# A two-stage fused kernel with twelve of its second-stage inputs turned by VectorE blocks and on-chip copies, and its first tile turned before its mean is known

## The chip, the cores and the metric

The kernel runs on one NeuronCore of one Trainium2 chip. The metric is the device time of one execution in microseconds, as the median of several runs. The profile is of one further execution, and its span is what the profiler saw between the first and the last instruction.

The engines are named as the profile names them: PE is TensorE's matmul stream and PEld its weight loads, DVE is VectorE, ACT is ScalarE, POOL is GpSimd, SP is SyncE. SP does no arithmetic here: it issues transfers from one queue, in order. POOL issues the indirect transfers (gathers of rows and scatters of rows). SBUF is the working memory of 128 partitions, and PSUM the memory into which PE writes.

## The reference, cut to what matters

There are 2048 tokens (4 x 512) of width 512, all in float32. A token's id chooses one of four experts by the thresholds 6250, 12500 and 18750. Each expert is one 512 x 512 matrix, which serves as gate, up and down matrix alike:

```
h  = layernorm(x)                       # no learned scale
g  = silu(h @ Wg[e].T);  u = h @ Wu[e].T
x  = x + tanh(g_xattn) * ((g * u) @ Wd[e].T)
```

The second stage is a feed-forward network over all tokens of the new x, with a router over eight experts, of which two are chosen:

```
h      = layernorm(x)
probs  = softmax(h @ wr.T); gates, idx = top 2, normalised
f      = silu(silu(h @ w1.T) @ w3.T) @ w2.T
out    = zeros; for k in 0, 1: out[idx[:, k]] += gates[:, k] * f
x      = x + tanh(g_ffn) * out
```

The index here is the expert's number, 0 to 7, and it is used as a row number. So the whole second stage adds up into rows 0 to 7 of the output, and the order in which tokens stand in it does not matter.

## The kernel before, in words

**Positions.** The kernel reads all token ids and works out, with DVE and small matmuls, a place for each token such that tokens of one expert lie together. `tok` (lines 274 to 278, sixteen small matmuls) gives for each of 17 passes of 128 places the token that sits there. `from_row` (L286) is the table for the gathers. `later`, `stepped` and `which` (L287 to L300) give for each unit its expert's matrix. `row_tables` (L308 to L323) gives the table for the scatters. While this runs, `busy` keeps PE occupied with matmuls whose result is not used.

**Passes.** Thirteen passes (0 to 12) hold 128 tokens of one expert each. Four more (13 to 16) hold four units of 32 places, each unit with its own matrix. A matrix is 1 MB; `load` issues it from SP into one of seven buffers (pool `mp`). SP first reads the expert's number from a table in SBUF (`which0` for the first pass, `held` for the others; `held` is a copy which POOL makes of `which`).

For each pass the work is: `gather` (POOL, L389); `centre` (DVE: moments of the row, mean taken off, L340 to L401); `turn_in` (PE transposes the 128 x 512 tile in four 128 x 128 pieces into PSUM, ACT copies it to `hT`); `up` (PE: z from hT and m, eight matmul records of 128 x 512; ACT: silu with the row's scale; DVE: the product g, L467); `turn_mid` (PE transposes g, ACT copies it to `gT`); `down` (PE: y; DVE adds the input row, L481; POOL scatters it to the output); `norms` (DVE: moments of the new row, L340, the inverse square roots of this row and of a later pass's input row with nine small instructions each, L355 to L373, and the scaled row `h_f`, L505); `turn_out` (PE transposes h_f into `tp_f`, ACT copies it to `hT2`, L515, or for passes 13 to 16 in four pieces at places read from a table, L527). `hT2` holds the second stage's input, features on partitions.

**The order of the work** is written out by hand; there is no scheduler. Each engine runs its own list in the order of the code. One turn i of the main loop (L876 to L909) issues `up` of pass i, `turn_in` of i + 1, `centre` of i + 2, `gather` and `load` of i + 3, `down` of i - 1, `turn_out` of i - 2, `norms` of i - 1, and `turn_mid` of i (positions in the list `order`, L383).

**The second stage** is taken in two blocks b of 1024 tokens. `sums_of_hT(b)` issues the router's products `lg` (PE, L699, two halves), then on DVE the difference T1, the 32 x 32 block transposes of the two `lg` (L710), and T2 to T4. `first_layer` is Strassen's scheme with seven products (X, Y, Z, L622), `second_layer` the products v (L730). These are cut into steps of 3.4 us of PE work each, and `step()` puts one step into the stream of passes. From turn 11 on there are two steps in a turn. Both `lg` and both X products lie in the pool `ps_x`, which has two PSUM buffers: X of a block takes the buffer of the first `lg` and can start only when that `lg` has been transposed by DVE. Before the change, `sums_of_hT(0)` stands at the end of turn 10, and the first step comes in turn 11, after that turn's z and y.

Of the kernel before, what the change touches and what calls it, by code (L numbers as in the profile page):

```python
# [19 lines left out]
P = 128  # L20
# [5 lines left out]
def tile_gated_moe_ffn(  # L26
# [39 lines left out]

    nc = tc.nc
# [17 lines left out]
    mp = ctx.enter_context(tc.tile_pool(name="mp", bufs=7))  # L85
    xp = ctx.enter_context(tc.tile_pool(name="xp", bufs=5))
# [13 lines left out]
        "idt", "pad", "psum", "padded", "lanes", "inpass",  # L100
# [12 lines left out]
    def load_w(src, name):  # L113
        w = ct_([P, KC, src.shape[1]], F32, name)
        nc.sync.dma_start(w, src.rearrange("(k p) f -> p k f", p=P))
        return w
# [148 lines left out]
    at_lane(0)  # L265
    what = ct_([P, NP, NJ], F16, "what")
# [6 lines left out]
    at_lane(1)  # L273
# [10 lines left out]
    busy(21)  # L284
# [20 lines left out]
    def row_tables():  # L305
# [18 lines left out]
            first, psum, float(-(NB - 1) * TB), float(TB), ALU.add, ALU.min  # L324
# [3 lines left out]
    hT2 = [ct_([P, KC, TB + (Q if b == NB - 1 else 0)], F32, f"hT2_{b}") for b in range(NB)]  # L328
# [9 lines left out]
    def moments(xt, name):  # L338
        st = small.tile([P, 6], F32, tag="st", name=f"st_{name}")
        nc.vector.bn_stats(st, xt)  # L340
        mv = small.tile([P, 2], F32, tag="mv", name=f"mv_{name}")
        nc.vector.bn_aggr(mv, st)
        return mv

    def inverse_roots(mvs_, names):


        n = range(len(names))

        def new(tag):  # L350
            return [small.tile([P, 1], F32, tag=tag, name=f"{tag}_{name}") for name in names]

        v, r, q, w, rs = new("v"), new("r"), new("q"), new("w"), new("rs")
        for i in n:
            nc.vector.tensor_scalar_add(v[i], mvs_[i][:, 1:2], EPS)  # L355
        for i in n:
            nc.vector.tensor_scalar(
                r[i].bitcast(I32), v[i].bitcast(I32), -0.5, float(0x5F3759DF), ALU.mult, ALU.add
            )
        for i in n:  # L360
            nc.vector.scalar_tensor_tensor(q[i], r[i], v[i], r[i], ALU.mult, ALU.mult)
        for i in n:
            nc.vector.tensor_scalar(w[i], q[i], 0.375, -1.25, ALU.mult, ALU.add)
        for i in n:
            nc.vector.tensor_scalar(w[i], w[i], q[i], 1.875, ALU.mult, ALU.add)
        for i in n:
            nc.vector.tensor_mul(r[i], r[i], w[i])
        for i in n:
            nc.vector.scalar_tensor_tensor(q[i], r[i], v[i], r[i], ALU.mult, ALU.mult)
        for i in n:  # L370
            nc.vector.tensor_scalar(q[i], q[i], -0.5, 1.5, ALU.mult, ALU.add)
        for i in n:
            nc.vector.tensor_mul(rs[i], r[i], q[i])  # L373
        return rs
# [8 lines left out]
    order = [0, 1, 2, 3, 4, 5, NF, 6, 7, 8, NF + 1, 9, 10, NF + 2, 11, 12, NF + 3]  # L383
    assert sorted(order) == list(range(NP))
    xs, x1s, mvs, rss, hs, hTs, gTs, gs, hs2, mats = {}, {}, {}, {}, {}, {}, {}, {}, {}, {}

    def gather(p):
        xt = xp.tile([P, D], F32, tag="x", name=f"x_{p}")
        nc.gpsimd.indirect_dma_start(  # L389
            out=xt,  # L390
            out_offset=None,
            in_=x,
            in_offset=bass.IndirectOffsetOnAxis(ap=from_row[:, p : p + 1], axis=0),
        )
        xs[p] = xt

    def centre(p):

        mvs[p] = moments(xs[p], f"a{p}")
        hs[p] = work.tile([P, D], F32, tag="h", bufs=4, name=f"h_a{p}")  # L400
        nc.vector.tensor_scalar(hs[p], xs[p], mvs[p][:, 0:1], None, ALU.subtract)  # L401

    def scale(*ps):
        for p, rs in zip(ps, inverse_roots([mvs.pop(p) for p in ps], [f"a{p}" for p in ps])):
            rss[p] = rs
# [6 lines left out]
    def first_in(p):  # L412

        st = small.tile([P, 6], F32, tag="st", name=f"st_a{p}")
        nc.vector.bn_stats(st, xs[p])
        mvs[p] = small.tile([P, 2], F32, tag="mv", name=f"mv_a{p}")
        nc.vector.bn_aggr(mvs[p], st)
        hTs[p] = work.tile([P, KC * P], F32, tag="hT", bufs=2, name=f"hT_{p}")
        n = D // 2
        for i in range(2):  # L420
            h = work.tile([P, n], F32, tag="h", bufs=4, name=f"h_a{p}_{i}")
            nc.vector.tensor_scalar(
                h, xs[p][:, i * n : (i + 1) * n], mvs[p][:, 0:1], None, ALU.subtract
            )
            tp = ps_tp.tile([P, n], F32, tag="tp", name=f"tp_a{p}_{i}")
            for k in range(n // P):
                nc.tensor.transpose(tp[:, k * P : (k + 1) * P], h[:, k * P : (k + 1) * P], ident)
            nc.scalar.copy(hTs[p][:, i * n : (i + 1) * n], tp)  # L428

    def load(p):  # L430

        n0, n = (p, 1) if p < NF else (NF + (p - NF) * G, G)
        mats[p] = []
        for i in range(n0, n0 + n):
# [9 lines left out]
            mats[p].append(m)  # L444
# [47 lines left out]
    def norms(p_in, p_out):  # L492
# [4 lines left out]
        xt = x1s.pop(p_out)  # L497
        mv = [moments(xt, f"f{p_out}")]
        names = [f"f{p_out}"]
        if p_in is not None:  # L500
            mv.append(mvs.pop(p_in))
            names.append(f"a{p_in}")
        rs = inverse_roots(mv, names)
        h = work.tile([P, D], F32, tag="h", bufs=4, name=f"h_f{p_out}")
        nc.vector.tensor_scalar(h, xt, mv[0][:, 0:1], rs[0], ALU.subtract, ALU.mult)  # L505
        hs2[p_out] = h
        if p_in is not None:
            rss[p_in] = rs[-1]

    def turn_out(p):  # L510

        tp = transposed(hs2.pop(p), f"f{p}").rearrange("p (k t) -> p k t", k=KC)
        if p < NF:
            b, t = divmod(p, TB // P)
            nc.scalar.copy(hT2[b][:, :, t * P : (t + 1) * P], tp)  # L515
            return
        for i in range(G):
            n = (p - NF) * G + i
            place = NF * P + n * Q - (NB - 1) * TB
# [3 lines left out]
                min_val=min(place - E * (Q - 1), TB),  # L523
                max_val=min(place, TB),
                skip_runtime_bounds_check_because="its place less at most E (Q - 1) pads, at most TB",
            )
            nc.scalar.copy(hT2[NB - 1][:, :, bass.ds(at, Q)], tp[:, :, i * Q : (i + 1) * Q])  # L527
# [47 lines left out]
    def sums_of_w1():  # L575

        h = D // 2
        a11, a12 = w1[:, 0:2, 0:h], w1[:, 2:4, 0:h]
        a21, a22 = w1[:, 0:2, h:D], w1[:, 2:4, h:D]
        ss = [ffp.tile([P, 2, h], F32, tag=f"S{i}", name=f"S{i}") for i in range(1, 5)]  # L580
# [10 lines left out]
    def sums_of_hT(b):  # L591
# [3 lines left out]
        b11, b12 = hT2[b][:, 0:2, 0:HB], hT2[b][:, 0:2, HB:TB]  # L595
        b21, b22 = hT2[b][:, 2:4, 0:HB], hT2[b][:, 2:4, HB:TB]
        ts = [ffp.tile([P, 2, HB], F32, tag=f"T{i}", name=f"T{i}_{b}") for i in range(1, 5)]
# [7 lines left out]
    def first_layer(b):  # L605
# [14 lines left out]
        def product(out_ps, a, bb, c, start):  # L620
            for k in range(2):
# [3 lines left out]
                    bb[:, k, :],  # L625
# [66 lines left out]
    def logits(b, half):  # L692
# [3 lines left out]
        for k in range(KC):  # L696
            cols = hT2[b][:, k, half * HB : (half + 1) * HB].rearrange("p (t c) -> p t c", t=TT)
# [127 lines left out]
    last = {b: max(i for i, p in enumerate(order) if min(p // (TB // P), NB - 1) == b) for b in range(NB)}  # L825
# [20 lines left out]
    load(order[0])  # L846
    gather(order[0])
    one = slice(order[1], order[1] + 1)
    nc.gpsimd.tensor_copy(held[0:1, one], which[0:1, one])
    load(order[1])  # L850
    for i in range(1, 5):
# [3 lines left out]
    first_in(order[0])  # L855
    scale(order[0])
    centre(order[1])
    scale(order[1])
    load(order[2])
    nc.sync.dma_start(gates[:, 0:1], g_xattn.to_broadcast([P, 1]))  # L860
    nc.sync.dma_start(gates[:, 1:2], g_ffn.to_broadcast([P, 1]))
    load(order[3])
    up(order[0], inside=lambda: turn_in(order[1]))
    centre(order[2])
# [8 lines left out]
    load(order[4])  # L873
# [89 lines left out]
```

## Time and profile before

| quantity | value |
|---|---|
| median time of 3 runs | 279.15 us (279.06 to 279.7) |
| the profiled execution's own time | 277.53 us |
| its span | 275.8 us |
| PE busy | 266.6 us (97% of the span) |
| DVE busy | 148.7 us (54%) |
| ACT busy | 69.3 us (25%) |
| PE transposes of h_f (tp_f), 68 records | 10.4 us in all |
| DMA moved | 42.54 MB |

The span leaves out 1.7 us of the execution's own time, and this execution was 1.6 us under the median of the three runs. Differences worked out in the span are therefore set against the span, and the result is then placed on the median. PE's matmul records overlap (a record of 0.595 us follows the last at 0.43 us), so the pieces of the chain of waits, which are counted from end to end, give the true cost of a piece of PE work.

### The profile page before, as it was taken

What the parts mean: (1) busy time and instruction counts of PE and PEld (TensorE: products, weight loads), DVE (VectorE), ACT (ScalarE), POOL (GpSimd) and SP (SyncE); (2) the same over time, 40 slices, a digit from 0 to 9 for tenths busy, and PEclk for the clock granted to TensorE, in tenths of its full rate; (3) what the DMA queues carried; (4) which work ended last, traced back from release to release, by engine and by line L of the source; (5) the groups of instructions that cost most, each with busy time, mean ns of one, the idle gap of its engine ahead of it and who ended that gap; (6) DMA issues with size and microseconds to landing.
All of it is one profiled execution on the core that took longest, in us unless ns stands there. A gap on an engine that the chain in (4) does not pass through costs nothing.

```text
span 275.8 us, 3562 instructions
## 1 busy us (share of the span) xinstructions
PE 266.6 (97%) x1173; PEld 125.4 (45%) x1173; DVE 148.7 (54%) x593; ACT 69.3 (25%) x134; POOL 39.3 (14%) x63
## 2 busy tenths in 40 slices
PE   5889999999999999999999999999999999999994
PEld 2445455544355454444344444534245444344362
DVE  6677877777888769918263481516253620711000
ACT  2022232232232231223143232312113233311120
POOL 6520122221122211211110010101010000000000
PEclk9999999999999999999999999999999999999999
DMA  0697998545669996697304084001000000000000
GB/s 1 217 354 277 408 402 334 173 155 206 228 225 402 389 409 258 173 398 264 112 26 166 2 312 180 38 0 40 0 12 2 0 0 1 0 0 2 0 0 2
DMA packets 20722, 42.54 MB, mean 154 GB/s; under 512 B 2143, under 2 KB 2207, under 8 KB 20704
## 3 DMA queue, kind: packets, MB, share of 16 engines
q1 hardware_dynamic: 17952, 33.66, 34.0%
q0 software_dynamic: 2720, 8.65, 8.3%
q8 instruction: 9, 0.15, 0.2%
q14 instruction: 9, 0.07, 0.1%
q10 hardware_dynamic: 32, 0.01, 0.0%
HBM read 38.10 MB, written 4.47 MB: 154 GB/s over the span
## 4 chain that ended last, share of the span: by engine, by line
PE 94%; DVE 2%; DMA 2%; issue 1%; ACT 0%; DVEq 0%
PE z L453 22%; PE y L453 21%; PE v L730 20%; PE X L622 10%; PE Y L622 5%; PE tp_f L380 3%; PE tp_a L380 3%; PE tp_g L380 3%; PE Z L622 2%; PE acc L742 1%; PE lg L699 1%; DMA x<-in_x_dram,from_row 1%; DMA idt<-in_ids_dram 1%; PE accT L758 1%; PE o L814 0%
## 5 line engine op out<-in xcount | busy, mean ns | idle before, releaser
L453 PE MATMUL z<-m,hT 128*32 128x512 f32 (+1 forms) x232 | 61.8, 595 | 0.2 <-ACT hT L428 0.2
L453 PE MATMUL y<-m,gT 128*32 128x512 f32 (+1 forms) x232 | 61.4, 594 | 0.0
L730 PE MATMUL v<-w,s 128*128 128x512 f32 (+1 forms) x136 | 57.3, 570 | 0.0
L730 PEld LDWEIGHTS v<-w,s 128*128 128x128 f32 x136 | 25.0, 190 | 27.2 <-issue 26.7
L453 PEld LDWEIGHTS z<-m,hT 128*32 128x32 f32 (+1 forms) x232 | 22.6, 146 | 29.5 <-issue 28.1
L453 PEld LDWEIGHTS y<-m,gT 128*32 128x32 f32 (+1 forms) x232 | 22.6, 146 | 27.8 <-issue 27.8
L482 POOL DMA_INDIRECT out_dram<-x,to_row x17 | 17.2, 1011 | 84.9 <-DVE x L481 82.7
L389 POOL DMA_INDIRECT x<-in_x_dram,from_row x17 | 16.7, 984 | 77.5 <-DVE h_a L401 22.9
L467 DVE SCALAR_TENSOR_TENSOR g<-z,rs_a,g 128x512 f32<-128x512 f32 x17 | 12.7, 750 | 27.1 <-ACT g L466 27.0
L466 ACT ACTIVATE g<-z,rs_a 128x512 f32<-128x512 f32 x17 | 11.7, 687 | 51.3 <-PE z L453 51.3
L481 DVE SCALAR_TENSOR_TENSOR x<-y,tg,x 128x512 f32<-128x512 f32 x17 | 12.7, 749 | 16.9 <-PE y L453 16.8
L738 ACT ACTIVATE s<-v 128x512 f32<-128x512 f32 (+1 forms) x17 | 9.7, 572 | 41.9 <-PE v L730 41.9
L515 ACT COPY hT<-tp_f 128x512 f32<-128x512 f32 x13 | 7.6, 587 | 43.5 <-PE tp_f L380 43.5
L340 DVE BATCH_NORM_STATS2 st_a<-x 128x6 f32<-128x512 f32 x16 | 11.0, 688 | 7.5 <-DMA x<-in_x_dram,from_row 7.5
L622 PE MATMUL X<-T,S 128*128 128x512 f32 x32 | 15.0, 592 | 0.0
L380 PEld LDWEIGHTS tp_f<-ident,h_f 128*128 128x128 f32 x68 | 8.2, 141 | 10.2 <-issue 10.2
L340 DVE BATCH_NORM_STATS2 st_f<-x 128x6 f32<-128x512 f32 x17 | 11.8, 695 | 0.6
L380 PEld LDWEIGHTS tp_a<-ident,h_a 128*128 128x128 f32 x64 | 7.7, 140 | 9.4 <-issue 9.1
L640 DVE TENSOR_TENSOR s<-X,c 128x512 f32<-128x512 f32 x4 | 2.8, 692 | 16.2 <-PE X L622 16.2
L473 ACT COPY gT<-tp_g 128x512 f32<-128x512 f32 x17 | 10.0, 586 | 5.3 <-PE tp_g L380 5.3
L380 PE MATMUL tp_f<-ident,h_f 128*128 128x128 f32 x68 | 10.4, 276 | 0.0
L380 PE MATMUL tp_g<-ident,g 128*128 128x128 f32 x68 | 10.2, 273 | 0.0
(165 smaller groups left out, 271.6 us busy)
## 6 DMA issues: line engine op xcount, KB each, us to landing
m<-in_ctxT_dram SPq DMA_DIRECT2D x29, 1024.0 KB
w<-in_w1T_dram SPq DMA_DIRECT2D x1, 1024.0 KB
w<-in_w3T_dram SPq DMA_DIRECT2D x1, 1024.0 KB
w<-in_w2T_dram SPq DMA_DIRECT2D x1, 1024.0 KB
x<-in_x_dram,from_row POOLq DMA_INDIRECT x17, 6.2
out_dram<-x,to_row POOLq DMA_INDIRECT x17, 6.1
wr<-in_wrT_dram SPq DMA_DIRECT2D x1, 64.0 KB
x_first<-out_dram SPq DMA_DIRECT2D x4, 4.0 KB
```

Of the source, the lines that this page charges most:

```text
L340: nc.vector.bn_stats(st, xt)
L380: nc.tensor.transpose(tp[:, k * P : (k + 1) * P], h[:, k * P : (k + 1) * P], ident)
L389: nc.gpsimd.indirect_dma_start(out=xt, out_offset=None, in_=x, in_offset=bass.IndirectOffsetOnAxis(ap=from_row[:, p : p + 1], axis=0),)
L453: nc.tensor.matmul(out_ps[i * n : (i + 1) * n, :], lhs[:, k * P + i * n : k * P + (i + 1) * n], m[:, k, :], start=(k == 0), stop=(k == KC ...
L466: nc.scalar.activation(g, z, AF.Silu, scale=rs)
L467: nc.vector.scalar_tensor_tensor(g, z, rs, g, ALU.mult, ALU.mult)
L473: nc.scalar.copy(gT, tp)
L481: nc.vector.scalar_tensor_tensor(xt, y, tg[:, 0:1], xt, ALU.mult, ALU.add)
L482: nc.gpsimd.indirect_dma_start(out=out, out_offset=bass.IndirectOffsetOnAxis(ap=to_row[:, p : p + 1], axis=0), in_=xt, in_offset=None, bou ...
L622: nc.tensor.matmul(out_ps, a[:, k, c * P : (c + 1) * P], bb[:, k, :], start=start and k == 0, stop=k == 1, skip_group_check=True,)
L730: nc.tensor.matmul(v, s1[:, k, c_b + t * P : c_b + (t + 1) * P], w3[:, k, c0 : c0 + n], start=(k == 0), stop=(k == KC - 1),)
L738: nc.scalar.activation(s2, v, AF.Silu)
```

## The change

Twelve of the seventeen passes (0 to 11) no longer have their second-stage input transposed by PE. In their place:

- ACT makes the scaled row h_f (`norm_out`) from a scale and a shift that DVE prepares; before, DVE made it.
- DVE transposes h_f in 32 x 32 blocks into a staging area (`turn_set`, one instruction for each pass). The staging areas are the two halves of `s1` for passes 0 to 3 and 4 to 7, and the buffer of `w2` for passes 8 to 11.
- SP then issues 16 copies within SBUF for each set of four passes (`exchange`), each of 32 partitions x 2 KB, which bring the blocks to the partitions where they belong. That makes 48 copies.
- `hT2` becomes three tiles for 512 tokens each, and a fourth that is filled by PE and ACT as before (passes 12 to 16).

The first pass's tile is transposed by PE as gathered. Meanwhile DVE sums each row, one matmul spreads the sums over all partitions, and DVE takes the mean off behind the transposition, in two halves. Its gather has a table of its own (`tok0`, `from_row0`), worked out ahead of the table for the other passes.

Also moved: the inverse roots are worked out for two columns at once in eleven instructions; `order` has the passes of four units later; `load` fills buffers as passes free them (`load_free`) and not three passes ahead; `xp` has six buffers, not five; `h` has three, not four; w1 is loaded one turn later, w3 in turn 12, w2 in turn 16; `sums_of_hT(0)` stands at the end of turn 11 with its first step right behind it, and turns 13 and 15 have a third step; one sum of w1 is written over its source; `busy(21)` is `busy(11)`.

```diff
+    what0 = ct_([P, NJ], F16, "what0")
+    nc.vector.scalar_tensor_tensor(what0, inpass, 0.0, number, ALU.is_equal, ALU.mult)
+    at_lane(1)
+    tok0 = ps_x.tile([P, 1], F32, tag="x", name="tok0")
+    for j in range(NJ):
+        nc.tensor.matmul(tok0, atlane[j // H][:, :, j % H], what0[:, j : j + 1], ...)
+    from_row0 = ct_([P, 1], I32, "from_row0")
+    nc.vector.tensor_scalar(from_row0, tok0, -1.0, 0.0, ALU.add, ALU.max)
     what = ct_([P, NP, NJ], F16, "what")
...
-    at_lane(1)
...
-    busy(21)
+    busy(11)
...
-    order = [0, 1, 2, 3, 4, 5, NF, 6, 7, 8, NF + 1, 9, 10, NF + 2, 11, 12, NF + 3]
+    order = [0, 1, 2, 3, 4, 5, 6, 7, 8, NF, 9, 10, NF + 1, 11, NF + 2, 12, NF + 3]
...
     def first_in(p):
+        raw = work.tile([P, KC * P], F32, tag="h", bufs=3, name=f"raw_{p}")
         for i in range(2):
...
+                nc.tensor.transpose(tp[:, k * P : (k + 1) * P], xs[p][:, c : c + P], ident)
+            nc.scalar.copy(raw[:, i * n : (i + 1) * n], tp)
+        total = small.tile([P, 1], F32, tag="total", name="total")
+        nc.vector.tensor_reduce(total, xs[p], AX.X, ALU.add)
+        spread = ps_y.tile([P, P], F32, tag="y", name="spread")
+        nc.tensor.matmul(spread, total.to_broadcast([P, P]), ident, start=True, stop=True)
+        for i in range(2):
+            nc.vector.scalar_tensor_tensor(hTs[p][:, half]..., spread..., -1.0 / D, raw[:, half]...,
+                ALU.mult, ALU.add)
+        mvs[p] = moments(xs[p], f"a{p}")
...
     def norms(p_in, p_out):
+        rs = inverse_roots(mv[:, 0:n, 1], f"f{p_out}")
+        if p_out < NS:
+            nc.vector.scalar_tensor_tensor(shift, mv[:, 0, 0:1], -1.0, rs[:, 0:1], ALU.mult, ALU.mult)
+            scaled[p_out] = rs[:, 0:1], shift
+            return
         nc.vector.tensor_scalar(h, x1s.pop(p_out), mv[:, 0, 0:1], rs[:, 0:1], ALU.subtract, ALU.mult)
...
+    def norm_out(p):
+        nc.scalar.activation(h, x1s.pop(p), AF.Identity, bias=shift, scale=rs)
+
+    def turn_set(p):
+        b, i = divmod(p, 4)
+        nc.vector.transpose(
+            turned_set(b).rearrange("p q (k i t) -> p k q i t", i=4, t=Q)[:, :, :, i, :],
+            hs2.pop(p).rearrange("p (k q t) -> p k q t", k=KC, q=4),
+        )
+
+    def exchange(b):
+        for q in range(4):
+            for g in range(G):
+                nc.sync.dma_start(
+                    hT2[b][q * Q : (q + 1) * Q, g].rearrange("p k c -> p (k c)"),
+                    turned_set(b)[g * Q : (g + 1) * Q, q, :],
+                )
...
     gather(order[0])
     one = slice(order[1], order[1] + 1)
+    gather(order[1])
     nc.gpsimd.tensor_copy(held[0:1, one], which[0:1, one])
-    load(order[1])
-    for i in range(1, 5):
+    load(1)
+    for i in range(2, 5):
         gather(order[i])
...
     for i in range(2, NP + 2):
+        before_last = order[i - 2]
         if i < NP:
             up(order[i])
         if i + 1 < NP:
             turn_in(order[i + 1])
+        if before_last < NS:
+            norm_out(before_last)
         if i + 2 < NP:
             centre(order[i + 2])
         if i + 3 < NP:
             gather(order[i + 3])
-            load(order[i + 3])
+        if before_last in (7, 11):
+            turn_set(before_last)
+        if before_last == 7:
+            exchange(1)
         if i <= NP:
             down(order[i - 1])
-        turn_out(order[i - 2])
+        load_free(i)
+        if before_last == 11:
+            exchange(2)
+        if before_last >= NS:
+            turn_out(before_last)
+        step()
         if i <= NP:
             norms(order[i + 2] if i + 2 < NP else None, order[i - 1])
-        step()
         if i > NP:
             step()
...
         if i < NP:
             turn_mid(order[i])
-        for b in range(NB):
-            if last[b] == i - 2:
-                hT_sums[b] = sums_of_hT(b)
-                running.append(ffn(b))
-        if last[0] != i - 2:
+        if i == 11:
+            hT_sums[0] = sums_of_hT(0)
+            running.append(ffn(0))
+        if i == NP + 1:
+            hT_sums[1] = sums_of_hT(1)
+            running.append(ffn(1))
+        step()
+        if before_last in hs2:
+            turn_set(before_last)
+            if before_last == 3:
+                exchange(0)
+        if i in (13, 15):
             step()
```

NS is 12, the number of passes that go the new way. `load_free(i)` loads, in the order of the units, as many matrices as there are buffers that passes before turn i have used up.

## Prediction

> **What bounds the kernel now.** I read the page first, then the chain of waits in order of time, then the timelines at the three places that the change touches: the start, the first `lg`, the last `lg`. The page:
>
> ```profile
> span 275.8 us, 3562 instructions
> PE 266.6 (97%) x1173; PEld 125.4 (45%) x1173; DVE 148.7 (54%) x593; ACT 69.3 (25%) x134; POOL 39.3 (14%) x63
> PE 94%; DVE 2%; DMA 2%; issue 1%; ACT 0%; DVEq 0%
> ```
>
> PE carries 94% of the chain. In time order the chain is PE's own list from 15.44 us (first z) to 271.3 us, piece after piece without a hole. So a PE piece removed there is worth its full length, and a wait put there costs its full length. First, the end of turn 10, chain and then DVE's timeline:
>
> ```profile
> 101.51 0.44 PE tp_f L380 x4
> 101.94 0.44 PE tp_g L380 x4
> 102.38 1.88 PE lg L699 x64
> 104.26 3.63 PE z L453 x8
> ```
>
> ```profile
> 101.79 0.74 DVE L481 SCALAR_TENSOR_TENSOR x<-y,tg,x 128x512 f32<-128x512 f32 x1
> 105.43 0.54 DVE L505 TENSOR_SCALAR h_f<-x,mv_f,rs_f 128x512 f32<-128x512 f32 x1
> 105.89 1.22 DVE L598 TENSOR_TENSOR T<-hT 128x1024 f32<-128x1024 f32 x1
> 107.03 0.50 DVE L710 STREAM_TRANSPOSE lt<-lg 128x128 f32<-128x128 f32 x2
> ```
>
> PE has finished `lg` at 104.26, but DVE transposes it only at 107.03, because the norms and T1 stand ahead of it. Nobody waits: the X that needs that PSUM buffer comes at 112.49, after a z, a tp_a and a y. The last `lg`, all engines:
>
> ```profile
> 207.24 0.60 PE L380 MATMUL tp_f<-ident,h_f 128*128 128x128 f32 x4
> 207.68 3.60 PE L730 MATMUL v<-w,s 128*128 128x512 f32 x8
> 209.22 0.27 ACT L527 COPY hT<-tp_f 128x128 f32 x1 [0.16 <-ACT hT L527]
> 209.52 1.23 DVE L598 TENSOR_TENSOR T<-hT 128x1024 f32<-128x1024 f32 x1 [5.32 <-ACT hT L527]
> 211.21 1.95 PE L699 MATMUL lg<-hT,wr 128*32 128x128 f32 x64
> ```
>
> A step of v covers the four ACT copies and T1. The start:
>
> ```profile
> 8.88 0.18 DVE L286 TENSOR_SCALAR from_row<-tok 128x17 int32<-128x17 f32 x1 [0.74 <-PE tok L276]
> 10.50 0.18 POOL L849 COPY held<-which 1x1 int32<-1x1 int32 x1
> 11.16 0.39 SPq L443 DMA_DIRECT2D m<-in_ctxT_dram  x1
> 15.44 2.84 PE L453 MATMUL z<-m,hT 128*128 128x512 f32 x6 [0.24 <-ACT hT L428]
> 19.44 0.30 PEld L453 LDWEIGHTS z<-m,hT 128*128 128x128 f32 x2 [0.69 <-ACT hT L410]
> ```
>
> The second pass's matrix is issued at 11.16; the trace has its completion at 19.33, 8.2 us later, amid four gathers. Its hT was ready at 19.35. So z of the second pass (19.70, that is 22.28, the start of tp_g, less six records at 0.43) began with the arrival of its matrix: hT is no later, and no earlier.
>
> [...] 303 ns for 128x128 f32 (L710). [...] The 8 KB of ids took 1.74 us from issue to use, but loads amid gathers take far longer (8.2 us above; gathers a median 6.2). [...] the page's clock row shows full speed throughout[...].
>
> **The change part by part** (against the profiled 275.8).
>
> *PE transposes removed.* Twelve passes x 0.437 us (the tp_f pieces; the 0.59 behind a y of four units moves to the next piece) = -5.24.
>
> *What replaces them, in the turns.* ACT: a copy of 0.59 goes, an activation of 0.69 with a scale (row L466) comes; ACT is 25% busy, nothing. DVE: h_f (0.54) goes, a block transpose comes. No row has 128x512 with a scattered output; between four times 303 = 1.2 us and 512 elements at the pace of h_f, 0.55 us; I take 0.6. Count a turn from the end of y: 0.07 to wake, product 0.77, statistics 0.73 + 0.22, roots 2.16 (nine alone take 1.90 at 201.75 to 203.65; two fused ones become two plain ones each: + 2 x (2 x 0.19 - 0.25)), shift 0.2, a sum of w1 0.62, transpose 0.6: 5.4. The next g waits for silu, 0.44 + 3.44 + 0.75 = 4.6 after the same y, ends at 6.15, and PE wants it at 7.76. So the turn has 1.6 us to spare, and even 1.2 us for the transpose costs nothing. Without this cover, each 0.1 over costs 0.1 in twelve turns.
>
> *Copies.* 48, on SP. Rows of direct issues are 0.28 to 0.49; 16 x 0.37 = 6 us a set. Queued behind are matrices. The tight one is set 1, in the turn in which pass 13 is z. From that z's end E: DVE is through with its transpose at E + 3.5 (silu 0.7, product 0.75, centre 1.4, transpose 0.6), SP with the copies at E + 9.5; the buffers of pass 13 come free only at E + 11.9. Pass 14 wants its matrices at E + 25.9. [...] Hidden. Bound above: rival B.
>
> *Stall 1, at the first X.* Its step now comes directly behind `lg` (end of turn 11). From y's end DVE needs 0.07 + 0.77 + 0.73 + 0.22 + 2.16 + 0.2, then T1 1.14, first transpose 0.30, PE's wake 0.04: 5.63 us. PE has tp_f 0.44, tp_g 0.44, lg 1.88 = 2.76. It waits 2.87, of which 0.19 is the delay that any matmul behind `lg` had before (3.63 against 3.44): +2.7. Behind it T2 to T4 and the add of Z are through before the next g; no further stall.
>
> *Stall 2, at the last `lg`.* Turns 11, 13 and 15 used up the steps, so nothing stands between the last tp_f and `lg`. Copies end 1.65 us after tp_f (207.84 to 209.49), then 0.03 + T1 1.14 + transpose 0.30 + 0.04: X at 3.16, where PE has 1.88 of `lg`. Wait 1.28, less 0.19: +1.1.
>
> *The start.* x_0: `tok0` begins at 7.3 and not 7.85, its gather at 8.8 and not 9.35, the rows arrive at about 12.4. But DVE now waits for PE twice, so `from_row` falls at 10.2 (+1.3), and the tables end at 13.0 and not 11.8: the row sum starts there, 13.65, spread 14.15, first half 14.6, z at 14.6 and not 15.44. Gain 0.8, if the second pass's z could follow. It needs its matrix: `which` + 1.3, and the gather of the second pass now stands ahead of the copy on POOL (0.97), so SP issues at 12.4 and not 11.16. The ramp then meets the gathers of passes 2 to 4 at their thickest (16.5 to 18.5 us). Bounds for its landing: 18.5 (5.2 us from issue were seen for the first matrix + 0.9) to 20.6 (8.2 us). I take 19.8: z of the second pass 0.45 later than before: +0.45. Bounds -0.8 and +1.2.
>
> *The rest* (sixth x buffer, third h buffer, w1 to w3 later, order of units): no PE wait follows from the lists of instructions and their waits. Bounds 0 to +0.5, taken at 0.
>
> Sum: -5.24 + 2.7 + 1.1 + 0.45 = -1.0, span 274.8. On the median: 279.15 - 1.0 = **278.2 us**.
>
> **The rivals.**
>
> *A. The start keeps its gain.* The second matrix lands by 18.5, since it may have been slowed by the gather of pass 1, which now runs ahead of it. For: the first matrix, alone, took 5.2 us. Against: three gathers still come on top. Start -0.8 in place of +0.45: time 276.9. Chance 0.2.
>
> *B. The copies hold up SP (slower).* The built program has SP wait before each copy for the transfer eight places earlier. If a copy takes 8 us to land, as the second matrix did, SP's pace is 1.0 us a copy, not 0.37. Set 1 then ends at E + 19.5, four matrices at E + 31.9, wanted at E + 28.6 with stall 1: +3.3, span 278.1, time 281.5. It decides from 0.8 us a copy, a landing of 6.4 us. For: gathers have a median of 6.2. Against: in slices 13 to 15 DMA has room. Chance 0.15.
>
> *C. The two stalls do not come* (DVE's order lets `lg` be transposed earlier): 274.4. Against: DVE's list has T1 and the norms ahead of it. Chance 0.05.
>
> *D. Something small everywhere:* transposes over 1.6 us, x rows late, PE slowed behind gaps: 279 to 280.5. Chance 0.1.
>
> **How the numbers follow.** The forecast case has 0.5, its own range 277.4 to 279.0. Within 0.3% (0.84 us, about what a measurement of this kernel can tell) is 278.31 to 279.99. Faster: A 0.2, C 0.05, a little over half of the forecast 0.27: 0.52. Same: the rest of the forecast 0.23, half of D 0.05, a mild B 0.02: 0.30. Slower: B 0.13, D 0.05: 0.18. Range 276.7 to 280.6: it leaves out C and the worse part of B.
>
> **What would show it.** Right: the first tp_f is that of pass 13, in turn 11; a hole of 2 to 3 us in PE ahead of the first X, released by DVE L813; a wait of about 1.1 us in two parts at the last `lg`; z of the second pass near 20.1; no PE wait on a matrix elsewhere. Wrong: PE waiting for m in the turn of pass 14 (B), a first X at once behind `lg` (C), tp_g waiting for g (DVE full), or a clock row below full.

## The result, and the profile after

The changed kernel takes 283.98 us as the median of five runs (281.43 to 287.51), where the kernel before takes 279.15 us. The ratio is 1.0146, with a 95% interval of 1.0116 to 1.0177; it leaves out the run of 287.51 us, which is 2.2% above the fastest and counts as slow. So the change made the kernel slower by 1.5%, where the prediction had 278.2 us. The profiled execution after took 283.98 us, with a span of 282.3 us (before 275.8). Single executions of one variant lie up to some 4 us from one another (e4: 279.98 to 283.88), and where their clocks differ (e2), 278.5 to 278.83 us goes with a mean granted clock of 0.996, and 280.32 to 282.73 with 0.98 to 0.986. So ratios carry their intervals, and each is to runs of the kernel before on the same chip. The clock is given as a share of full speed; "half clock" is a granted clock of 0.50, and a "hole" is a stretch in which PE waits.

The page after: busy time, PE's slices, the granted clock, the chain's shares.

```profile
PE 268.4 (95%) x1133; PEld 122.1 (43%) x1133; DVE 150.2 (53%) x510; ACT 71.9 (25%) x134; POOL 39.4 (14%) x63
...
PE   5889999999999996699999999999999999999994
...
PEclk9799999999999999979999999999999999999998
...
PE 86%; DMA 9%; DVE 1%; SPq 1%; issue 1%; POOL 0%; ACT 0%; ACTq 0%; POOLq 0%
```

PE's row has a hole in slices 16 and 17 (106 to 120 us), the clock row has a 7 right behind it, and DMA carries 9% of the chain (before 2%). The timeline of PE there (start, duration, engine, line, work, and in brackets the idle time ahead and what ended it):

```profile
102.52 3.60 PE L510 MATMUL y<-m,gT 128*128 128x512 f32 x8
...
112.09 1.98 PE L725 MATMUL X<-hT,w 128*128 128x512 f32 x4 [1.46 <-DVE lt L813]
...
115.72 1.05 PE L510 MATMUL z<-m,hT 128*32 128x512 f32 x4
117.45 1.05 PE L510 MATMUL z<-m,hT 128*32 128x512 f32 x2 [0.67 <-DMA m<-in_ctxT_dram]
120.16 5.23 PE L510 MATMUL z<-m,hT 128*32 128x512 f32 x26 [1.67 <-DMA m<-in_ctxT_dram]
```

Two things stand one behind the other. The first X comes 5.95 us after the end of y (106.14 in the chain of waits). Then z of pass 14 waits for its third and for its fourth matrix, and its last 26 records take 5.23 us. In all, this z takes from 115.72 to 125.38, 9.66 us where a z of four units takes 3.57. The stretches of four microseconds (PE, PEld, DVE, ACT and POOL busy, granted clock, DMA share, GB/s) say why the last part is slow:

```profile
112.00:116.00 4.00, 3.91 (x10) 1.58 (x12) 3.71 (x6) 0.59 (x1) 0.00 (x0) 1.00 1.04 401
116.00:120.00 4.00, 1.82 (x6) 0.14 (x2) 0.59 (x1) 0.00 (x0) 0.00 (x0) 1.00 1.04 388
120.00:124.00 4.00, 3.84 (x24) 0.97 (x25) 0.00 (x0) 0.00 (x0) 0.00 (x0) 0.57 0.90 334
```

DMA runs full here (a share of 1.02 from 106 to 112 us, 1.04 from 112 to 120), so what can make the matrices late is when they were asked for, and how many bytes are in the way; the experiments separate the two. And behind the holes the clock falls to half (0.50 from 120.0 to 123.4 us). SP's queue, and its line for the copies (min/median/max in ns):

```profile
90.49 11.21 SPq L605 DMA_DIRECT2D hT<-s  x16
102.48 3.62 SPq L492 DMA_DIRECT2D m<-in_ctxT_dram  x4
```

```profile
L605 SPq DMA_DIRECT2D hT<-s x32: 507/589/1754, 64.1 to 101.1; - x32
```

The 16 copies of the second set hold SP from 90.49 to 101.7 us. The first matrix of pass 14 takes the buffer of pass 8, whose last reader y ends at 90.3; the other three take buffers of pass 13, free at 98.2. All four are asked for only from 102.48 on. Without these copies (run e2 below), SP asks for the first at 90.51 and for the second at 98.37:

```profile
90.51 8.23 SPq L492 DMA_DIRECT2D m<-in_ctxT_dram  x2
```

The other two places, the last lg and the start:

```profile
215.76 0.60 PE L404 MATMUL tp_f<-ident,h_f 128*128 128x128 f32 x4
...
219.54 1.98 PE L725 MATMUL X<-hT,w 128*128 128x512 f32 x4 [0.42 <-DVE lt L813]
```

```profile
9.92 4.04 PE L205 MATMUL idle<-ones 128*128 128x512 bf16 x11
...
15.39 2.84 PE L510 MATMUL z<-m,hT 128*128 128x512 f32 x6 [0.59 <-DVE hT L463]
...
20.12 1.10 PE L510 MATMUL z<-m,hT 128*128 128x512 f32 x2 [0.59 <-DMA m<-in_ctxT_dram]
```

The sum over the span, before to after: start +0.4 (z of the second pass at 20.12, before 19.70); twelve PE pieces -5.24; first X +3.0 (5.95 - 2.76 of PE work - 0.19); z of pass 14 +6.1; last lg +1.1. That is +5.4 of the measured +6.5. The other 1.1 lies in small pieces, not all of them followed up: the first records after a wait (X 1.98 in place of 1.72, z of the second pass), and pieces behind products of four units (0.15 to 0.19 each).

### The profile page after: what moved, and what is told of

It reads as the page before. It is cut to its first block, busy times and chain, and to the rows that moved or that the text cites. A ratio compares the mean times of both kernels' runs of the same rounds, so it can differ in the third digit from the quotient of the medians.

```text
span 282.3 us, 3480 instructions
## 1 busy us (share of the span) xinstructions
PE 268.4 (95%) x1133; PEld 122.1 (43%) x1133; DVE 150.2 (53%) x510; ACT 71.9 (25%) x134; POOL 39.4 (14%) x63
## 4 chain that ended last, share of the span: by engine, by line
PE 86%; DMA 9%; DVE 1%; SPq 1%; issue 1%; POOL 0%; ACT 0%; ACTq 0%; POOLq 0%
PE z L510 20%; PE v L833 20%; PE y L510 20%; PE X L725 9%; DMA m<-in_ctxT_dram 8%; PE Y L725 5%; PE tp_g L404 3%; PE tp_a L404 2%; PE Z L725 2%; PE idle L205 2%; PE acc L845 1%; PE tp_f L404 1%; PE accT L861 1%; DMA idt<-in_ids_dram 1%; PE o L917 0%
## 5 line engine op out<-in xcount | busy, mean ns | idle before, releaser
L510 PE MATMUL z<-m,hT 128*32 128x512 f32 (+1 forms) x232 | 65.5, 625 | 3.5 <-DMA m<-in_ctxT_dram 2.9
L524 DVE SCALAR_TENSOR_TENSOR g<-z,rs_f,g 128x512 f32<-128x512 f32 x14 | 10.2, 726 | 29.9 <-ACT g L523 29.9
L523 ACT ACTIVATE g<-z,rs_f 128x512 f32<-128x512 f32 x14 | 9.6, 688 | 48.5 <-PE z L510 45.7
L725 PE MATMUL Y<-T,w 128*128 128x512 f32 x32 | 15.0, 592 | 0.0
L404 PEld LDWEIGHTS tp_g<-ident,g 128*128 128x128 f32 x68 | 8.3, 141 | 9.1 <-issue 9.1
L366 DVE BATCH_NORM_STATS2 st_a<-x 128x6 f32<-128x512 f32 x17 | 11.6, 681 | 0.0
L743 DVE TENSOR_TENSOR s<-X,c 128x512 f32<-128x512 f32 x4 | 2.8, 692 | 14.2 <-PE X L725 14.2
L443 ACT COPY hT<-tp_a 128x512 f32<-128x512 f32 x16 | 9.3, 580 | 3.7 <-PE tp_a L404 3.7
```

Of the source, the lines that this page charges most:

```text
L510: nc.tensor.matmul(out_ps[i * n : (i + 1) * n, :], lhs[:, k * P + i * n : k * P + (i + 1) * n], m[:, k, :], start=(k == 0), stop=(k == KC ...
L523: nc.scalar.activation(g, z, AF.Silu, scale=rs)
L524: nc.vector.scalar_tensor_tensor(g, z, rs, g, ALU.mult, ALU.mult)
L725: nc.tensor.matmul(out_ps, a[:, k, c * P : (c + 1) * P], bb[:, k], start=start and k == 0, stop=k == 1, skip_group_check=True,)
```

## The experiments

The theory after this reading: SP is held by *issuing* the copies, so pass 14's matrices come late; stall 1 and the half clock add to it. The rivals: it is the copies' bytes in the DMA engines; or the matrices are late by themselves; or stall 1 alone is the cause. (Stall 1 is the wait ahead of the first X, stall 2 the one at the last lg.)

### Relieving SP alone, filling holes, undoing one set

e1_pool_half: `exchange(1)` takes two queues.

```diff
-                nc.sync.dma_start(
+                eng = nc.gpsimd if b == 1 and q >= 2 else nc.sync
+                eng.dma_start(
```

> The second set's 16 copies are split: SP issues 8, POOL's queue the other 8; bytes and everything else as in the changed kernel (about 283.0 us). Queue theory (SP is held by issuing copies, so the matrices of the second pass of four units are issued 4 to 12 us late): SP is through at about 95.5 and not 101.7 us, the wait for m and the stretch at half clock behind it go, worth up to 6.1 us: 276.5 to 278. Bandwidth theory (the copies' traffic fills the DMA engines, whoever issues them): no change, 282 to 284. If POOL's issues hold up scatters or gathers: above 284.

280.87 us against 277.82, ratio 1.014 (1.0092 to 1.0189). PE's timeline:

```profile
111.95 3.57 PE L726 MATMUL X<-hT,w 128*128 128x512 f32 x4 [3.19 <-DVE lt L814]
...
117.17 3.64 PE L510 MATMUL z<-m,hT 128*32 128x512 f32 x32
```

The mechanism answers as expected: SP is through at 96.2, and z of pass 14 runs its 32 records without a wait. But the gain does not come out: the hole ahead of X is there in full (3.19 us), and X takes 3.57 us, at half clock (0.50 from 111.8 to 115.2). The median lies between the two ranges that were expected.

e2_no_set1: `exchange(1)` left out.

```diff
-        if before_last == 7:
-            exchange(1)
...
-            return hT2[b].rearrange("p g k c -> p k g c")
+            return hT2[0 if b == 1 else b].rearrange("p g k c -> p k g c")
```

> The 16 copies of the second set are left out; whatever reads that set's tile reads the first set's instead (the output for passes 4 to 7 is not the reference's). It prices these copies together, issue and traffic. Queue theory and bandwidth theory alike: the whole 6.1 us comes back, 276.5 to 277.5. If it lies above 280, pass 14's matrices were late for another reason (their buffers, their own 1 MB each). Compared with the run that has the copies split: the difference is what the traffic costs.

280.32 us, ratio 1.0097 (1.0061 to 1.0133). The expected 6.1 us do not come back. The profiled execution (278.5 us, a granted clock of 1.00 from 110 to 172 us) has no wait for m, but y's end to X is 5.96 us with a wait of 3.22 us. So the matrices are in time without the copies, and what stays is stall 1. The eleven executions fall in two groups: five at a mean granted clock of 0.996 take 278.5 to 278.83 us, six at 0.98 to 0.986 take 280.32 to 282.73. The first group is thus only 0.3% above the kernel before (the changed kernel's execution at a clock of 1.000 in e8 is 1.4% above), and the median depends on how many executions lose the clock.

e4_pe_set1: passes 4 to 7 by `turn_out` again, no second set of copies.

```diff
-        if before_last in (7, 11):
+        if before_last == 11:
             turn_set(before_last)
-        if before_last == 7:
-            exchange(1)
...
-        if before_last >= NS:
+        if before_last >= NS or before_last // 4 == 1:
             turn_out(before_last)
```

> One part undone: passes 4 to 7 are transposed by PE and copied by ACT as before the change, and the second set's copies are gone; the first and third sets stay. Queue theory: 6.1 us come back, four PE pieces of 0.437 us go: 283.0 - 6.1 + 1.75 = 278.6 (278.2 to 279.2). If the late matrices had nothing to do with the copies: about 284.8.

281.72 us, ratio 1.0153 (1.0086 to 1.022), 3 us above the expectation. Again no wait for m; X waits 3.15 us and then takes 3.22 us (113.43 to 116.65), most of it at half clock (0.50 from 114.0 to 117.5).

e3_fill: five idle matmuls in the holes of the changed kernel.

```diff
+    def fill(n):
+        for _ in range(n):
+            nc.tensor.matmul(acc, ident, hT2[0][:, 0].rearrange("p k c -> p (k c)"), start=True, stop=True)
...
             for i, m in enumerate(mats[p]):
+                if filler and k == 0:
+                    fill(filler[i])
...
             running.append(ffn(0))
+            fill(2)
```

For pass 14, `filler` is (0, 0, 1, 2).

> Five matmuls whose result is not used are put into PE's holes of the changed kernel: two between lg and the first X, one ahead of the third unit of pass 14 and two ahead of the fourth. Nothing else moves; the waits for m stay. If the half clock from 120.0 to 123.4 us comes from the holes ahead of it: the clock row stays full, and of the 1.7 us lost there 1.2 to 1.7 come back: 281.3 to 281.9. If it does not: 283 to 284, as five matmuls of 0.43 us in waits of 1.5, 0.7 and 1.7 us cost at most 0.9.

283.04 us, ratio 1.0211 (1.0173 to 1.0248): worse. The price was wrong: such a matmul is two records, 0.86 us and not 0.43, so 4.3 us went into 3.8 us of holes, and the last part of z began at 120.60. The clock was full there in the profile (1.00 from 110 to 172 us), but the changed kernel once more, below, had it full too. This run settles nothing.

### Both waits, one at a time and together

e5_norms_late: in turn 11 the norms stand behind T1 and the transposes of lg.

```diff
-        if i <= NP:
+        if i <= NP and i != 11:
             norms(order[i + 2] if i + 2 < NP else None, order[i - 1])
...
         lts[b] = [turned(b, half, lg) for half, lg in enumerate(lgs)]
+        if between is not None:
+            between()
...
-            hT_sums[0] = sums_of_hT(0)
+            hT_sums[0] = sums_of_hT(0, lambda: norms(order[13], order[10]))
```

> Against the changed kernel one thing: in turn 11 the norms (about 3.4 us of DVE) stand behind T1 and the two transposes of lg, not ahead of them; the copies stay on SP. X is then free to start about 3 us earlier, at once behind lg. Theory that the two waits lie in series: pass 14's last matrix still lands near 119 to 120 us, so what the first X gains is waited for at m: no gain, within 1 us of the changed kernel, and the half clock stays. Rival (each wait costs by itself): 3 us and more come back.

283.3 us, ratio 1.0165 (1.0133 to 1.0197): no gain, as the theory of waits in series says.

```profile
115.87 1.91 PE L510 MATMUL z<-m,hT 128*32 128x512 f32 x2 [2.91 <-DMA m<-in_ctxT_dram]
118.58 5.65 PE L510 MATMUL z<-m,hT 128*32 128x512 f32 x26 [0.80 <-DMA m<-in_ctxT_dram]
```

X starts at once behind lg (107.84); what it gains is waited for at m, and the half clock stays (0.50 from 115.9 to 122.7; the last part of z takes 5.65 us).

e6_split_norms: e1 and e5 together.

> Both: the second set's copies split between SP and POOL, and the norms of turn 11 behind the transposes of lg. With the matrices in time at about 112.4 us and X at about 109: the 3.2 us of stall 1 go, and with them the half clock in the 3.4 us behind it (1.7 us): on a chip where the kernel before takes 277.8 us, 276 (275.5 to 277.5). If pass 14's last matrix, needed near 114, is late again, up to 2 us less gain.

277.73 us against 278.87, ratio 0.9958 (0.9935 to 0.9981): faster than the kernel before. Of m a wait of 0.83 us is left, and the clock stays full there (1.00 from 100 to 120 us):

```profile
114.12 3.62 PE L510 MATMUL z<-m,hT 128*32 128x512 f32 x26 [0.83 <-DMA m<-in_ctxT_dram]
```

e7_all: e6, a step fewer in turn 15, and `held` copied ahead of the second pass's gather.

```diff
-        if i in (13, 15):
+        if i == 13:
...
-    gather(order[1])
     nc.gpsimd.tensor_copy(held[0:1, one], which[0:1, one])
+    gather(order[1])
```

> As the last, and two more places put back in the manner of the kernel before: turn 15 has no third step, so a step stands between the last tp_f and the last lg (stall 2, 1.3 us); and POOL copies the second pass's number into held ahead of gathering that pass's rows (its matrix is issued about 1 us earlier, z of the second pass 0.4 to 0.8 us earlier). Sum: 1.7 to 2.1 us below the last: 274.2 where the kernel before takes 277.8. If the second matrix lands no earlier for it (three gathers run by then): 274.8.

281.16 us, ratio 1.007 (1.0045 to 1.0095): worse than e6, and both edits show why. A line of the chain at the start, and one of PE's timeline at the last z:

```profile
11.97 6.21 DMA x<-in_x_dram,from_row
```

```profile
182.36 4.05 PE L510 MATMUL z<-m,hT 128*32 128x512 f32 x20 [2.14 <-DMA m<-in_ctxT_dram]
```

The copy of `held` starts at 11.63 in either order, since it waits for `which`. So the gather in front of it was free; behind it, its rows land at 18.2, and the second pass runs 1.2 us later (its tp_g at 23.93, in the changed kernel's second run 22.68). Not all of this is the gather: in this execution the idle matmuls at the start took 4.86 us, not 3.81 as in e8. In two runs that keep the gather in front and have idle matmuls as slow (e9 and e17), this tp_g comes 0.6 and 0.8 us earlier than here. And the third step of turn 15 was the cover for the last pass's matrices: without it, PE waits 2.14 us for m, and the clock is 0.50 from 182.5 to 185.9.

e8_after: the changed kernel again.

> The changed kernel itself, once more, beside the others on the same chip: 1.4% above the kernel before (1.1 to 1.8), with X first at 112 us, a wait for m in pass 14 and a stretch of half clock behind it.

282.38 us, ratio 1.015 (1.0097 to 1.0203). The profiled execution waits for m to 119.81, but its clock stays full (1.00 from 100 to 227 us): its 26 records take 3.62 us, against 5.23. So the half clock is 1.6 us, in some executions, behind the same holes (here 1.37, 0.58 and 1.67 us).

### Small parts, and all of the transposes

e9_lt_first (e6, with the transposes of lg ahead of T1), e10_tail (e9, with two of the last pass's four copies on DVE), e11_act (e9, with copies SP 4, ACT 4, POOL 8):

```diff
-        nc.vector.tensor_sub(ts[0], b12, b11)
         lts[b] = [turned(b, half, lg) for half, lg in enumerate(lgs)]
+        nc.vector.tensor_sub(ts[0], b12, b11)
```

```diff
+            by_dve = p == order[-1] and i % 2 == 1
...
+            if by_dve:
+                nc.vector.tensor_copy(to, part)
+            else:
+                nc.scalar.copy(to, part)
```

```diff
+                eng = (nc.scalar, nc.sync, nc.gpsimd, nc.gpsimd)[q] if b == 1 else nc.sync
+                eng.dma_start(
```

> The version with split copies and late norms, and DVE transposes both lg ahead of T1 (both blocks). At the last lg the first X then waits for the second half of lg only, not for T1: of stall 2's 1.3 us some 0.6 go, and nothing else moves: ratio to the kernel before 0.9936 where that version had 0.9958 (0.992 to 0.9955).

> The same, and the last pass's four copies out of PSUM go half to ACT and half to DVE, which is idle there; lg's second half then finds its input about 0.85 us earlier and stall 2 is gone: 0.5 to 0.7 us below the version before it, ratio 0.9915. If DVE's read of a place from the table costs more than ACT's: no gain.

> Split copies, late norms, lg ahead of T1, and four of the second set's sixteen copies issued by ACT (SP 4, ACT 4, POOL 8). SP is through 2.4 us earlier, the first matrix of pass 14 is issued at 94 and not 97 us, and the 0.8 us wait for pass 14's last matrix goes: ratio 0.9915. If ACT's four issues (2.4 us) delay its copy of gT: up to 1 us slower than that version instead.

Ratios 1.0052 (1.0031 to 1.0073), 1.0009 (0.9993 to 1.0025) and 0.9969 (0.9949 to 0.9989). The edit of e9 costs in the first block: T1 and what is behind it on DVE slide, and y at 119.13 waits 0.47 us for `s` (1.07 in e11). That does not explain all of e9's distance to e6, which ran on another chip; this stays open. So two kernels that differ in this edit alone lie 0.9% apart on two chips, and not all of it has a known cause. Within the three, which ran together, the split of the tail copies is worth 0.4% and four copies on ACT 0.8%.

e12_pe_all: no block transposes and no copies at all, the rest as changed.

```diff
-            turn_set(before_last)
-            exchange(1)
-            exchange(2)
-            exchange(0)
-        if before_last >= NS:
-            turn_out(before_last)
+        turn_out(before_last)
```

> One part undone: all twelve passes are transposed by PE and copied by ACT again, no block transposes, no copies; the order, the loads, the steps, the first tile and the two-column roots stay as changed. It prices what came along with the transposes: start 0.4, stall 1 3.2, stall 2 1.3, some 0.5 in small pieces, and half clock in some runs: 5 to 6.5 us above the kernel before, ratio 1.018 to 1.024. The DVE transposes and copies as built are then worth only what lies between this and the changed kernel's 1.015. If it comes to 1.01 or less, the stalls cost less than their length and the copies more.

284.76 us, ratio 1.0254 (1.0212 to 1.0297), above the expected range. So what came along with the transposes costs about 2.5%, and the transposes by DVE with their copies, as built, bring about 1% back (on different chips). The profiled execution (282.64 us) shows the 3.00 us wait at X, no wait for m and a full clock (1.00 from 100 to 147 us); it lies 1.85% above the kernel before, within the expected range. The slower runs have no profile.

### What of the copies costs, what lowers the clock, and the best of it

e14_none_late: e2 and e5 together.

> The second set's 16 copies left out (its readers read the first set; the output for passes 4 to 7 is not the reference's) and the norms of turn 11 behind the transposes of lg. The floor for any way of issuing those copies: neither a wait for m in pass 14 nor stall 1: ratio to the kernel before 0.990 (0.987 to 0.994).

275.52 us against 277.48, ratio 0.991 (0.9887 to 0.9933), as expected.

e15_short_late: as e14, with 16 copies of 256 bytes a partition on SP.

```diff
+        n = D if b != 1 else 64
...
-                    turned_set(b)[g * Q : (g + 1) * Q, q, :],
+                    turned_set(b)[g * Q : (g + 1) * Q, q, 0:n],
```

> The same, but SP issues all 16 copies, each of 32 partitions x 256 bytes and not 2 KB (an eighth of the bytes, the same count and the same instructions on SP; readers as in the last, so the output is not the reference's). Queue theory (what costs is SP being held about 11 us): pass 14's matrices are as late as with whole copies, ratio near 1.0165 (1.010 to 1.019). Bandwidth theory (what costs is 1 MB of copies in the DMA engines): ratio as without copies, 0.990 to 0.996. In between, both count by where it falls.

0.9928 (0.99 to 0.9956). This did not test what it was meant to: the short copies read columns that passes 4 and 5 write, so SP began at 84.03 and was free at 95.7, though it was held for 11.63 us. Holding SP cost little or nothing here (0.9928, where no copies gave 0.991), and it ended before most of the buffers came free: the first matrix is asked for at 96.23, and z of pass 14 does not wait. With columns that pass 7 writes, beside whole copies on the same chip:

```diff
-                    turned_set(b)[g * Q : (g + 1) * Q, q, 0:n],
+                    turned_set(b)[g * Q : (g + 1) * Q, q, D - n :],
```

> As the run with copies of 256 bytes a partition, which had read columns that only passes 4 and 5 write, so that SP began them 6 us earlier; now they read columns that pass 7 writes and begin at 90 like the whole copies. Same count, an eighth of the bytes (readers read the first set's tile, so the output is not the reference's). Queue theory: SP is through at about 101, pass 14's last matrix lands near 117, ratio 1.010 to 1.019, beside the whole copies' run on this chip. Bandwidth theory: ratio 0.990 to 0.996.

> The counterpart on the same chip: whole copies on SP, norms of turn 11 late, once more. Ratio as in its first run, 1.0165 (1.012 to 1.020).

1.0096 (1.0061 to 1.0131) with short copies, 1.019 (1.0139 to 1.024) with whole ones. SP's timeline with short copies:

```profile
90.66 10.62 SPq L606 DMA_DIRECT2D hT<-s  x16
102.52 7.73 SPq L492 DMA_DIRECT2D m<-in_ctxT_dram  x6
```

An eighth of the bytes holds SP nearly as long (whole copies: 11.04 us in e18). Against no copies at all (0.991, on another chip) the hold costs 1.9%, 5.2 us, with the little traffic of the short copies in it; the other bytes add 0.9%, 2.6 us. In the two profiles the last part of z begins at 118.03 and at 119.34 (1.3 us apart), and the half clock lasts 3.4 and 6.8 us. So neither theory takes all: the hold has about two thirds of it. The intervals leave the share open by a good deal, not the order.

e16_fill_split: e1, with three idle matmuls in the hole ahead of X.

```diff
             running.append(ffn(0))
+            fill(3)
```

> The version with split copies, stall 1 left as it is (3.2 us), and three matmuls whose result is not used (2.6 us of PE) in that hole. X starts no earlier. If the hole is what lowers the clock behind it, the clock is full from 108 to 125 us in the profile, and the median falls by 1 to 1.7 us: ratio 1.005 to 1.009 where that version had 1.014. If the clock falls for another reason: 1.012 to 1.016.

279.48 us, ratio 1.0066 (1.0049 to 1.0082), where e1 had 1.014.

```profile
110.39 2.84 PE L505 MATMUL acc<-hT,ident 128*128 128x512 f32 x6
113.71 1.98 PE L732 MATMUL X<-hT,w 128*128 128x512 f32 x4 [0.47 <-DVE lt L820]
```

X comes 5.47 us after the first lg (5.39 in e1), so no earlier, but takes 1.98 us and not 3.57. From the first lg to z of pass 14 it is 9.10 us here and 10.61 in e1: useless work in the hole makes the kernel faster. The granted clock is 1.00 from 108 to 120 us here, and in e1 it is 0.60 from 112 to 116. That fits the hole as what lowers the clock in e1. But not every hole of this length goes with a fall: behind 3.22 us in e2 and 3.00 us in e12 the clock of the profiled execution stayed at 1.00. What decides that is not shown.

e13_best: e6, copies SP 4, ACT 4, POOL 8, tail copies split, and T1 ahead of the transposes of lg in block 0 but behind them in block 1.

```diff
+        if b == 0:
+            nc.vector.tensor_sub(ts[0], b12, b11)
         lts[b] = [turned(b, half, lg) for half, lg in enumerate(lgs)]
+        if b == 1:
+            nc.vector.tensor_sub(ts[0], b12, b11)
```

> What helped, together: the second set's copies issued SP 4, ACT 4, POOL 8; norms of turn 11 behind T1 and the transposes of lg (T1 first in the first block, so that y does not wait for s; the transposes first in the second); the last pass's four copies half on DVE. Sum against the version with SP 4, ACT 4, POOL 8 (0.997): 1.1 us of y's wait and 0.5 of stall 2 less: ratio 0.991 (0.988 to 0.995).

275.18 us (273.61 to 276.34) against 277.48, ratio 0.9915 (0.9885 to 0.9946): 0.85% faster than the kernel before.

```profile
109.02 1.98 PE L736 MATMUL X<-hT,w 128*128 128x512 f32 x4
...
112.65 3.64 PE L510 MATMUL z<-m,hT 128*32 128x512 f32 x32
```

X stands behind lg and z of pass 14 behind Z, both without a wait. The ratios that carry the verdict:

| second set's copies | norms ahead, as changed | norms behind |
|---|---|---|
| 16 on SP | 1.0146 and 1.015 | 1.0165 and 1.019 |
| 16 short ones on SP | not run | 1.0096 |
| 8 on SP, 8 on POOL | 1.014 | 0.9958 |
| none | 1.0097 | 0.991 |

By the medians, either cure alone gains little or nothing; both together gain 1.9% (e5, e6 and e8 ran on one chip: 1.0165, 0.9958 and 1.015; the other rows mix chips).

## Why the prediction was wrong, point by point

- **PE transposes removed, -5.24:** right. From y to y a full turn takes 7.75 us (40.15 to 47.90), before 8.19 (39.94 to 48.13).
- **What replaces them in the turns:** right. The block transpose takes 0.704 us (0.6 taken), and nothing waits for it.
- **Copies, "Hidden":** the step that failed, in three terms. SP began at E + 4.2 (3.5 taken; E is 86.3). Its 16 copies took 11.2 us, not 6: 0.589 us each by the median, 0.63 from one to the next, and one of 1.75, where 0.37 had been read off the issue of a matrix. So SP was done at E + 15.4 and not E + 9.5, behind the buffers (E + 11.9) and not ahead of them. The sum counts three loads of 2.6 us behind the buffers. The first matrix of pass 14 needs none of these buffers (e2 asks for it at 90.51), but held by the copies, all four went out together. And from SP's first load to the last of the four it took 17.6 us (102.48 to about 120.1; 15.5 in e17, 16.6 in e6), not the 12.4 that rival B counts. Of these, 10.4 are four loads at 2.6 us, which the trace before shows (409 GB/s from 26 to 32 us, 1.05 MB a load); what was added to them for a landing was the author's estimate, and no run here separates it.
- **Rival B** named the place and the direction, by another cause. It has SP waiting for copies to land, at 1.0 us a copy; measured are 0.70 with 2 KB a partition, 0.63 for the last ten, and 0.66 with 256 bytes (10.62 us for sixteen in e17), so SP's time hardly depends on their bytes, which speaks for the issue itself and against the landing. It held that it decides only from 0.8; it decided earlier, since the loads took longer than its 12.4 us. It had a chance of 0.15 and priced 3.3 us; this z lost 6.1.
- **Clock:** the prediction names a clock row below full as a sign against it, but no term of its sum prices one; before, the mean granted clock is 1.000. Here the clock fell to 0.50 behind a hole of 3.19 us (e1) and one of 2.14 us (e7), and behind shorter ones in a row (after: 1.46, 0.67, 1.67), though not in every execution (e2: 3.22; e8: 1.37, 0.58, 1.67). It costs 1.6 us where it strikes (26 records in 5.23 us, in e8 in 3.62).
- **Stall 1, +2.7:** right in kind and a little small: 5.95 us from y to X, and 5.96 without the copies (e2), 5.63 taken. Of the difference, 0.18 us is the roots (2.34 us in e2, 2.16 taken) and 0.17 the way from the shift to T1 (0.37 us, most of it in DVE's queue; 0.2 taken).
- **Stall 2, +1.1:** right: 3.17 us from tp_f to X (3.16 taken).
- **The start, +0.45:** right in its result (20.12; 20.15 taken), with luck and for partly wrong reasons. The first z came at 15.39 and not 14.6: the eleven idle matmuls took 4.04 us, with a granted clock of 0.50 from 10.8 to 14.2 (4.70 us for twenty-one before; in e7 4.86 for eleven at a granted 1.00). In four profiles in which they take 2.54 us (e2, e4, e12, e13) it came at 14.64 to 14.69, as the sum has it. But the matrix set the end anyway, and its landing varies: with this start unchanged, z of the second pass begins at 19.66 in e6 and at 21.43 in e16. And the gather ahead of `held` cost nothing (e7).
- **The rest, 0:** no wait came from it; but the third step in turn 15, which the sum booked only as the cause of stall 2, was cover for a load (e7).

What is left without the failed step: e2's profile has no copies of the second set and a clock of 1.00 from 110 to 172 us, and its 278.5 us stand against 277.8 before (a median), +0.7, where the sum says -1.0. Of these 1.7 us, by estimate from its pieces, stall 1 is 0.3, the first records behind the waits 0.5, the very end 0.4 (3.9 us from the last product to the end of the span, before 3.5), the second pass 0.1, and the rest, not followed up, probably pieces behind products of four units.

## What to carry to other kernels

Price a queue's issues by rows of the same kind of transfer, and then ask what stands behind them in that queue: here 16 small copies, 0.6 us each, held back 4 MB of loads. Where two waits stand in series, test the cures together, since each alone shows little. And a hole in a busy PE can cost more than its length: behind 3.19 us in e1 the clock was 0.50, and X took 3.57 us, where it took 1.98 at a clock of 1.00 with the hole filled (e16).

## What the runs showed of the hardware that was not expected

- A copy of 32 partitions x 2 KB within SBUF cost SP 0.589 us of issue (median of 32 in the changed kernel), and a 1 MB load 0.373 (median of 29). Sixteen copies of 256 bytes a partition held SP for 10.62 us (e17), sixteen of 2 KB for 11.04 (e18).
- The clock fell to half behind a hole of 3.19 us in e1 and of 3.15 us in e4, but not behind 3.22 us in e2 or 3.00 us in e12. Where it was seen to fall between the first z and the last product, it stayed there for 3.4 us (the changed kernel, e1, e4, e7, e17) or for 6.8 us (e5, e18). Filling the hole with unused matmuls won 0.7% (e16 against e1, on two chips).
- The block transpose of 128x512 f32 with a scattered output took 0.704 us (median of twelve in the changed kernel).
